# GAT source exponentials: spread over the partitions by DMA through a DRAM scratch, instead of by matmuls and copies

## Chip, cores, metric

The kernel runs on one core of one Trainium2 chip. The metric is the time of one execution in device microseconds (us).

## The reference

`x` is 16 batches of 1024 nodes by 256 channels, `adj` a 1024 x 1024 adjacency. Four layers follow one another, each on a layer norm of `x` and added to `x`. Layers 0, 1 and 3 are graph attention (GAT); layer 2 is a transformer block with the adjacency as mask.

```python
# layers 0 and 1 (one head), layer 3 the same for 4 heads of 64 channels
h = matmul(relu(layernorm(x)), W)
e = leaky_relu((h @ a1)[:, :, None] + (h @ a2)[:, None, :])   # source of row i + target of column j
att = softmax(where(adj > 0, e, -big), axis=-1)
x = x + act(matmul(att, h))                                   # relu or elu
```

With `s = h @ a1` and `d = h @ a2`, exp(leaky_relu(s_i + d_j)) is, up to a factor of i that cancels in the softmax, max(exp((alpha-1) s_i), exp((1-alpha) d_j)) * exp(alpha d_j). The kernel computes the three exponentials once per node. Each weight then is one max and one multiply with the mask.

## The kernel before

The exponentials `e` come out with the nodes on the partitions. For the weights, the targets j stay on the partitions, but the source values of 512 rows i have to lie along the free dimension, the same on all partitions: a row `r`. Making `r` is the part that the change replaces.

```python
        def see_gat(s):                       # once a stage, when the last e is there
            H = s.heads
            i = {0: 0, 1: B, 3: 2 * B}[s.layer] + s.b
            nc.gpsimd.tensor_copy(s.v[:, :, :, s.hs], s.e[:, :, 2 * H :])
            # ... two reductions for a range check

        def gat_front(s, n, h, box):          # one item: 512 rows of one head
            # ...
            def spread_source():
                rp = ps_sc.tile([P, HALF], F32, tag="sc", name="rp")
                for i in range(TH):           # 4 matmuls of 128 columns: column of e, made wide, times identity
                    nc.tensor.matmul(
                        rp[:, i * P : (i + 1) * P], lhsT=s.e[:, n * TH + i, h : h + 1].to_broadcast([P, P]),
                        rhs=ident, start=True, stop=True,
                    )
                box["r"] = work.tile([P, HALF], F32, tag="r", name="r", bufs=2)
                nc.scalar.copy(box["r"], rp)

            def weights(j):                   # 8 an item, on VectorE
                # ...
                nc.vector.scalar_tensor_tensor(
                    box[j // 2][:, j % 2, :], box["r"], s.e[:, j, H + h : H + h + 1], mask[:, j, cols], ALU.max, ALU.mult
                )
            return [spread_source] + [lambda j=j: weights(j) for j in range(NT)]

        def gat_back(s, n, h, box):           # 4 groups of 8 products: 257 columns (one head) or 65 (layer 3)
            # ...
                    nc.tensor.matmul(
                        av[:, : s.hs + 1], lhsT=box[j // 2][:, j % 2, i * P : (i + 1) * P], rhs=s.v[:, j, h, :],
                        start=(j == 0), stop=(j == NT - 1),
                    )
        # ...
        for i, (s, front, _) in enumerate(items):        # when each piece is emitted
            lead = 1 if s.layer == 2 else 8 if s.heads == 1 else 4
            for f, piece in enumerate(front):
                slot = first_slot[i] - lead + f * lead // len(front)
                (early if slot < 0 else due[slot]).append((s, piece))
        # ...
            for fs, piece in due[at_slot]:
                settle(fs)                    # drains the way in of stage fs before its first piece
                piece()
```

A *stage* is one layer of one batch. Stages of two batches alternate: layers 0, 1, 2, 3 of b and b+1, a *pair*, eight pairs in all. The *way in* of a stage (statistics, norm, transpose, projection, exponentials) is emitted in small steps between the products of the stage before. `settle` emits at once whatever of it is left.

## Time and profile before

In what follows PE is TensorE (PEld its weight loads), DVE VectorE, ACT ScalarE, POOL GpSimd and SP SyncE. `av` are the products, `rp` the spreads, `pm` the projections and `tp` transposes, by the names of the tiles that they write. Each fp32 matmul leaves two records in a trace, so a group of 8 products is 16 records.

| | before |
|---|---|
| median (lowest to highest) | 5569.73 us (5540.11 to 5572.35), 3 runs |
| profiled run | 5551.8 us, granted clock 0.951 |
| PE, DVE, ACT busy | 90%, 71%, 34% |

The prediction below shows the chain, the stretches of one pair and the groups concerned. The row of granted clock in the view of 40 slices (tenths of full speed, 9 is 90% or more):

```profile
PEclk9999999999999999998999999998999999999998
```

### The profile page before, as it was taken

What the parts mean: (1) busy time and instruction counts of PE and PEld (TensorE: products, weight loads), DVE (VectorE), ACT (ScalarE), POOL (GpSimd) and SP (SyncE); (2) the same over time, 40 slices, a digit from 0 to 9 for tenths busy, and PEclk for the clock granted to TensorE, in tenths of its full rate; (3) what the DMA queues carried; (4) which work ended last, traced back from release to release, by engine and by line L of the source; (5) the groups of instructions that cost most, each with busy time, mean ns of one, the idle gap of its engine ahead of it and who ended that gap; (6) DMA issues with size and microseconds to landing.
All of it is one profiled execution on the core that took longest, in us unless ns stands there. A gap on an engine that the chain in (4) does not pass through costs nothing.

```text
span 5551.8 us, 71153 instructions
## 1 busy us (share of the span) xinstructions
PE 4978.5 (90%) x27266; PEld 3127.0 (56%) x27266; DVE 3932.2 (71%) x7928; ACT 1905.7 (34%) x3345; POOL 1437.2 (26%) x2120
## 2 busy tenths in 40 slices
PE   4988899879998899988999889998899988999888
PEld 3832598226972279622795228852288423983248
DVE  4557885668757687576875678756786567865777
ACT  2344323442234422344223441234413443234430
POOL 1213322223222232123331232312323033231330
PEclk9999999999999999998999999998999999999998
DMA  2000000000000000000000000000000000000000
GB/s 79 1 1 1 3 29 1 1 1 5 27 1 1 1 7 26 1 1 1 16 16 1 1 1 16 16 1 1 1 16 16 1 1 1 20 5 1 1 1 17
DMA packets 40714, 45.92 MB, mean 8 GB/s; under 512 B 4144, under 2 KB 39088, under 8 KB 40368
## 3 DMA queue, kind: packets, MB, share of 16 engines
q1 hardware_dynamic: 35200, 37.75, 2.0%
q8 instruction: 218, 3.57, 0.3%
q10 hardware_dynamic: 5168, 3.54, 0.3%
q14 instruction: 128, 1.05, 0.1%
HBM read 24.51 MB, written 16.78 MB: 7 GB/s over the span
## 4 chain that ended last, share of the span: by engine, by line
PE 62%; DVE 30%; ACT 5%; issue 1%; POOL 1%; DVEq 0%; DMA 0%; ACTq 0%; POOLq 0%
PE av L561 25%; PE pm L461 14%; DVE pe L646 13%; PE sc L638 9%; PE acc L657 8%; DVE p L548 5%; ACT pe L644 4%; PE tp L456 3%; PE rp L538 3%; DVE st L445 2%; DVE y L713 1%; PE tpo L681 1%; DVE y L750 1%; DVE y L596 1%; DVE y L712 1%
## 5 line engine op out<-in xcount | busy, mean ns | idle before, releaser
L561 PE MATMUL av<-v,p 128*128 128x65 f32 (+1 forms) x12288 | 1968.5, 314 | 11.9 <-DVE y L596 10.5
L561 PEld LDWEIGHTS av<-v,p 128*128 128x128 f32 x12288 | 1748.4, 196 | 129.3 <-PE av L561 12.7
L646 DVE TENSOR_TENSOR pe<-pe,mask_pos 128x1024 f32<-128x1024 f32 x1024 | 1235.4, 1247 | 727.2 <-ACT pe L644 726.2
L644 ACT ACTIVATE pe<-sc 128x1024 f32<-128x1024 f32 x1024 | 992.9, 1022 | 767.8 <-PE sc L638 759.8
L657 PE MATMUL acc<-pe,v 128*33 128x512 f32 x4096 | 1058.4, 640 | 0.0
L449 POOL TENSOR_SCALAR rstd<-stats 128x1 f32<-128x1 f32 x768 | 411.4, 536 | 2410.7 <-DVE stats L447 2076.7
L548 DVE SCALAR_TENSOR_TENSOR p<-r,e,mask_pos 128x512 f32<-128x512 f32 x1280 | 917.3, 750 | 85.6 <-ACT r L543 84.6
L638 PE MATMUL sc<-qT,kT 32*128 32x512 f32 x4096 | 664.7, 708 | 0.0
L450 POOL TENSOR_TENSOR rstd<-rstd,minus_half 128x1 f32<-128x1 f32 x768 | 618.9, 806 | 64.0
L657 PEld LDWEIGHTS acc<-pe,v 128*33 128x33 f32 x4096 | 204.5, 115 | 674.0 <-issue 477.9
L461 PE MATMUL pm<-l_wx,hT 128*128 128x259 f32 (+1 forms) x1536 | 435.9, 410 | 11.8 <-ACT hT L457 11.8
L461 PEld LDWEIGHTS pm<-l_wx,hT 128*128 128x128 f32 x1536 | 288.5, 199 | 153.4 <-ACT hT L457 66.8
L574 DVE RECIPROCAL inv<-av 128x1 f32<-128x1 f32 x768 | 125.7, 164 | 320.1 <-PE av L561 315.8
L456 PE MATMUL tp<-ident,xn 128*128 128x128 f32 x1024 | 201.1, 281 | 156.2 <-DVE xn L473 146.5
L689 POOL TENSOR_TENSOR y<-y,z 128x256 f32<-128x256 f32 x128 | 100.7, 787 | 923.2 <-DVE z L685 923.2
L493 ACT ACTIVATE e<-pm 128x3 f32<-128x3 f32 (+1 forms) x384 | 67.5, 176 | 759.1 <-PE pm L461 759.1
L638 PEld LDWEIGHTS sc<-qT,kT 32*128 32x128 f32 x4096 | 186.5, 198 | 237.0 <-issue 146.5
L456 PEld LDWEIGHTS tp<-ident,xn 128*128 128x128 f32 x1024 | 130.0, 147 | 301.8 <-issue 117.5
L457 ACT ACTIVATE hT<-tp 128x256 f32<-128x256 f32 x512 | 194.5, 383 | 257.2 <-PE tp L456 257.2
L456 PE MATMUL tp<-ident,y 128*128 128x128 f32 x256 | 64.0, 337 | 230.9 <-DVE y L713 230.9
L473 DVE TENSOR_SCALAR xn<-x,stats,rstd 128x256 f32<-128x256 f32 x512 | 248.5, 485 | 14.8 <-PE tp L456 8.3
L543 ACT COPY r<-rp 128x512 f32<-128x512 f32 x192 | 112.2, 585 | 403.0 <-PE rp L538 331.2
(83 smaller groups left out, 4215.3 us busy)
## 6 DMA issues: line engine op xcount, KB each, us to landing
x<-in_x_dram SPq DMA_DIRECT2D x16, 1024.0 KB, 5.2
out_dram<-x SPq DMA_DIRECT2D x64, 256.0 KB, 2.1
edges<-in_adj_dram SPq DMA_DIRECT2D x8, 512.0 KB, 5.0
qkv_sb<-in_L_gnn_w_qkv_dram ACTq DMA_DIRECT2D x1, 768.0 KB, 6.5
l_wx<-in_L_gnn_W_dram ACTq DMA_DIRECT2D x2, 256.0 KB, 4.1
ab<-in_L_gnn_a_dram ACTq DMA_DIRECT2D x4, 128.0 KB, 4.1
w_sb<-in_L_gnn_w_dram ACTq DMA_DIRECT2D x2, 256.0 KB, 6.9
g_sb<-in_L_gnn_ln_g_dram ACTq DMA_DIRECT2D x2, 128.0 KB, 6.5
```

The costliest lines, as they stand in the source:

```text
L449: nc.gpsimd.tensor_scalar(r, stats[:, 1:2], EPS, None, ALU.add)
L450: nc.gpsimd.tensor_tensor(r, r, minus_half, ALU.pow)
L456: nc.tensor.transpose(tp[:, k, :], src[:, k * P : (k + 1) * P], ident)
L457: nc.scalar.activation(dst[:, :, t * P : (t + 1) * P], tp, func)
L461: nc.tensor.matmul(dst, lhsT=lhsT[:, k, :], rhs=rhs[:, k, :], start=(k == 0), stop=(k == KC - 1))
L473: nc.vector.tensor_scalar(xn, xs[s.b][:, t, :], box["m"], box["r"], ALU.subtract, ALU.mult)
L548: nc.vector.scalar_tensor_tensor(box[j // 2][:, j % 2, :], box["r"], s.e[:, j, H + h : H + h + 1], mask[:, j, cols], ALU.max, ALU.mult)
L561: nc.tensor.matmul(av[:, : s.hs + 1], lhsT=box[j // 2][:, j % 2, i * P : (i + 1) * P], rhs=s.v[:, j, h, :], start=(j == 0), stop=(j == NT ...
L638: nc.tensor.matmul(sc[:, hh, :], lhsT=s.kT[r0 : r0 + D2, g, j * P : (j + 1) * P], rhs=s.qT[r0 : r0 + D2, g, cols], start=True, stop=True,)
L644: nc.scalar.activation(p, sc, AF.Exp, scale=SCALE2)
L646: nc.vector.tensor_tensor(p, p, m, ALU.mult)
L657: nc.tensor.matmul(s.acc[pair][hh * 64 : hh * 64 + D2 + 1, :], lhsT=s.v[:, j, h, :], rhs=box[pair][:, hh, :], start=(j == 0), stop=(j == N ...
```

## The change

The intent is to free TensorE of 768 small matmuls and ScalarE of 192 copies: a stage's source exponentials are written to a DRAM scratch as rows, and each row is read back with a stride of 0 over the partitions. Since a DMA was expected to take longer to land than the matmuls and the copy, the read is issued 4 (one head) or 3 (four heads) slots before the old place of the spread; a slot is one group of products in layer 3 and half a group in layers 0 and 1.

```diff
+        dram = ctx.enter_context(tc.tile_pool(name="dram", bufs=3, space=bass.MemoryType.DRAM))
...
+                    self.rows = dram.tile([self.heads, N], F32, tag="rows", name="rows")
...
         def see_gat(s):
+            for h in range(H):
+                nc.sync.dma_start(
+                    out=s.rows[h : h + 1, :].rearrange("o (t p) -> p (o t)", p=P), in_=s.e[:, :, h]
+                )
...
             def spread_source():
-                rp = ps_sc.tile([P, HALF], F32, tag="sc", name="rp")
-                for i in range(TH):
-                    nc.tensor.matmul(
-                        rp[:, i * P : (i + 1) * P], lhsT=s.e[:, n * TH + i, h : h + 1].to_broadcast([P, P]),
-                        rhs=ident, start=True, stop=True,
-                    )
                 box["r"] = work.tile([P, HALF], F32, tag="r", name="r", bufs=2)
-                nc.scalar.copy(box["r"], rp)
+                nc.sync.dma_start(out=box["r"], in_=s.rows[h : h + 1, cols].to_broadcast([P, HALF]))
...
             lead = 1 if s.layer == 2 else 8 if s.heads == 1 else 4
+            if s.layer != 2:
+                slot = first_slot[i] - lead - (4 if s.heads == 1 else 3)
+                (early if slot < 0 else due[slot]).append((s, front.pop(0)))
```

## The prediction

> **What bounds the kernel now.** Sixteen batches go in eight pairs; each pair passes layer 0 (b, b+1), layer 1, layer 2, layer 3, so one pair takes about 690 us of the 5551.8. I read first the busy tenths in slices, which repeat eight times, then the chain that ended last, then the table of stretches for one pair, since the averages (PE 90%, DVE 71%) mix stages with different limits.
>
> From the page, the chain:
>
> ```profile
> PE 62%; DVE 30%; ACT 5%; issue 1%; POOL 1%; DVEq 0%; DMA 0%; ACTq 0%; POOLq 0%
> PE av L561 25%; PE pm L461 14%; DVE pe L646 13%; PE sc L638 9%; PE acc L657 8%; DVE p L548 5%; ACT pe L644 4%; PE tp L456 3%; PE rp L538 3%; DVE st L445 2%; DVE y L713 1%; PE tpo L681 1%; DVE y L750 1%; DVE y L596 1%; DVE y L712 1%
> ```
>
> The matmuls that the change removes (rp, L538) stand on it with 3%; the copy that follows them (L543) does not appear. Where they stand is told by the table of stretches of one pair. Its columns are the stretch and its length, then busy us of PE, PEld, DVE, ACT, POOL, the granted clock, DMA share, GB/s. The four rows are layer 3 of batch b, layer 3 of b+1, the layers 0 and 1 of the next pair (their first 179 us), and layer 2.
>
> ```profile
> 628.00:717.00 89.00, 81.98 (x612) 76.28 (x611) 77.31 (x200) 17.93 (x46) 34.17 (x51) 0.96 0.02 7
> 717.00:791.00 74.00, 73.15 (x618) 72.22 (x618) 68.41 (x165) 15.03 (x36) 12.08 (x17) 0.98 0.09 30
> 791.00:970.00 179.00, 178.21 (x873) 147.48 (x873) 106.99 (x261) 53.90 (x139) 48.64 (x83) 1.00 0.03 10
> 980.00:1300.00 320.00, 269.64 (x1244) 84.29 (x1240) 226.31 (x338) 142.84 (x186) 83.62 (x111) 0.93 0.00 1
> ```
>
> Layers 0 and 1 are bound by PE alone (178.2 of 179; DVE 60%): a PE microsecond saved there is saved. Layer 3 is bound by PE and DVE together (b: 92 and 87%; b+1: 99 and 92%): what PE gives up is soon asked for by DVE. Layer 2 hardly has this change in it.
>
> The groups and waits that the change touches:
>
> ```profile
> L538 PE MATMUL rp<-ident,e 128*128 128x128 f32 x1536 | 219.2, 290 | 8.9 <-ACT pe L644 8.9
> L543 ACT COPY r<-rp 128x512 f32<-128x512 f32 x192 | 112.2, 585 | 403.0 <-PE rp L538 331.2 <-DVE p L548 62.5 <-DVE st L445 6.1
> L548 DVE SCALAR_TENSOR_TENSOR p<-r,e,mask_pos 128x512 f32<-128x512 f32 x1280 | 917.3, 750 | 85.6 <-ACT r L543 84.6
> DVE p L548 <- ACT r L543: 116.1, 105, 2.0
> ```
>
> and PE in order in layer 1:
>
> ```profile
> 836.48 0.38 PE L456 MATMUL tp<-ident,xn 128*128 128x128 f32 x2
> 836.70 1.06 PE L538 MATMUL rp<-ident,e 128*128 128x128 f32 x8
> 837.59 1.91 PE L561 MATMUL av<-v,p 128*128 128x257 f32 x8
> ```
>
> The sum 219.2 us counts overlapping ends. From start to start one spread costs PE 837.59 - 836.70 = 0.89 us, with 192 of them 171 us, which is the chain's 3%. The last wait line says that DVE stood 116 us, 105 times, waiting for a spread row; 1.1 us each.
>
> **What the Trainium skill says.** "DMA: Bandwidth & Descriptors", Rules for kernel authors: a strided last dimension becomes one descriptor per element. So one write of a row (1024 values of 4 B, out of a strided tile) is 1024 packets. No DMA before has this in volume. The same page, Anatomy of one DMA, gives a fixed cost of about 2 us, mostly the receipt; the trace agrees in kind (32 KB broadcasts of ab land in 3.0 us, 256 KB stores in 2.1, 256 KB loads of l_wx in 4.1). The same page, Two DMAs through the same engine are not ordered: a read of what a DMA wrote has to wait for the completion semaphore, so write and read add up. The instruction list of the changed kernel shows such waits on each first read; no run yet gives the time. "TensorE: Matmul & The Clock Gate", Part 1: PE idleness lowers the clock for a window. The trace agrees: after 0.85 us of PE idle at 740.1 us the next spread took 1.98 us instead of 1.06, and that 10 us stretch shows 0.83. Small waits in layer 3 thus cost more than their length.
>
> **The change part by part.**
>
> *Removed from PE, layers 0 and 1.* 2 spreads per batch and layer, 4 x 16 = 64, times 0.89 us = 57 us, in a PE-bound stage: gain 57.
>
> *Removed from PE and DVE, layer 3.* 8 spreads per batch, 128 in all, 114 us of PE time. But in b+1 DVE has 68.4 us of work in 74: at best 5.6 us can go, I take 4. In b, most slices are DVE-bound by the tail of layer 2, with PE full only around 660 to 680; DVE waits for r there only 1.6 us; I take 3. Together 7 us x 8 pairs = 56. The ceiling, DVE at 100% in b+1 and 5 in b, would be 85.
>
> *Removed at the seam of layers 2 and 3.* rp borrows a score buffer; PE waited for ACT before it 24.4 us in 16 places, and the spread itself sits in the latency chain of layer 2. I take 15, choosing not to add all of it since the next score matmul inherits part of the wait.
>
> *Removed from ACT.* 192 copies of 0.585 us = 112 us; ACT is at 34% and not on the path: 0 by itself.
>
> *Added, DMA.* 96 row writes and 192 reads of 256 KB (50 MB). The scalar queue's 5168 mostly small packets took 0.1% of 16 engines' span, 89 us, or 17 ns each (9 to 26 with the rounding). A row is 64 packets per engine, 1.1 us (up to 1.7); landing about 3.0 + 1.1 = 4 us; four rows about 7.4. A read is estimated at 3 to 5 us. In the steady state r of an item can be asked for when DVE ends the item two before, and is needed one item later: 8 products of 0.72 us and 4 pairs of small operations of 0.4 us, 7.3 us. That hides it, save when a 1 MB load of x (5.2 us) is ahead in the rings.
>
> *Moved: the slot of the spread.* It is issued 4 slots (one head) or 3 slots (four heads) earlier, and a stage's way in must be finished (the schedule is drained) before its first spread. In layer 1 this pulls two steps of the way in together: PE waits for one transpose to be copied, about 0.7 us, twice a pair: 8 pairs x 1.4 = 11, and about 6 once at the start. In layer 3 of b+1 six steps are drained at once instead of three, so a chain statistics, POOL (1.55 us), norm, transpose, projection stands bare: about 3 us x 8 = 24. (Before, this drain already cost DVE about 4 us at 714.)
>
> *Added wait.* After that drain come 4 writes of rows and the first read behind them: 7.4 + some 3 us, against some 5 to 7 us of DVE work left of the item before. About 4 us x 8 = 32. For layer 3 of b, and for layer 0, the rows are long written: 0. For layer 1 there are 4 slots of about 2.2 us plus DVE slack: 0.
>
> Sum: -57 - 56 - 15 + 11 + 6 + 24 + 32 = -55. I shade it to -60, since the clock should gain a little with the shorter couplings, and predict 5570 - 60 = 5510 us.
>
> **The rivals.** (a) *Full gain*: all 171 us of rp and part of the 116 us of DVE waits go, since the PE-to-ACT-to-DVE round trip in every item was the true bound of layer 3. For it: the waits are exposed in front of DVE. Against: DVE is busy 92% in b+1, so the waits are worth 6 us a pair. It would give some 5420, faster by 2.7%. (b) *DMA latency takes the place of the wait*: if the element-wise row writes cost several times my 17 ns, or if reads land in over 7 us, DVE would wait for r at each item of layer 3. For it: thousands of 4-byte packets have no precedent in this trace. Against: the reads are long rows, and two buffers give a whole item of lead. With 2 us on each of 128 items it would be +256, minus the 57 of layers 0 and 1 and the seam: about 5700. (c) *DVE is the bound in layer 3 and nothing is gained there*, with the settling cost paid: -57 - 15 + 73, the time of before within 0.2%.
>
> **Range and chances.** Between (c) at about 5570 and a little under the ceiling of layer 3 without added waits (-57 - 85 - 15 + 17 = -140, 5430) lies most of what I hold likely; with run to run scatter of half a per cent (5540 to 5572) I set 5430 to 5580. Two per cent is 111 us: faster than 5458 needs layer 3 near its ceiling and a free seam, 0.2. Slower by 2% needs (b) in full: 0.07. Within 2%: 0.73.
>
> **What would show each step right or wrong.** In the changed profile: layers 0 and 1 of a pair still have PE at 99% and are shorter by about 7 us less 1.4 (the right sign of the first term). Layer 3 of b+1: length 74 falls to some 70, DVE busy goes to 95% or more, PE drops under 95%; if PE stays at 99% and the stretch is 66, rival (a) holds. The waits list must have no "DVE p <- ACT r"; in its place there should be a wait of DVE for the DMA of r, with few entries (about one per pair, 3 to 5 us each); a hundred entries would be rival (b). The landing of rows should be about 4 us for one and 7 to 8 for four; over 12 us proves my packet estimate wrong. The drain at the end of layer 3 of b should show DVE idle of 6 to 8 us where it had 4. The prediction goes wrong mostly by the cost of 4-byte packets and by how far DVE-bound slices of layer 3 give back what PE saves.

## The result, and the profile after

The changed kernel takes 6107.82 us (median of 4 runs, 6094.63 to 6112.29) against 5567.05 us (4 runs) before: ratio 1.0978, 95% interval 1.0939 to 1.1018. It is slower by 9.8%, and the prediction's range ends 528 us below it. Ratios here are the mean time of one kernel's fast runs over that of the other's of the same rounds, so not quite the ratio of the medians quoted.

The granted clock and the chain, from the page of the kernel after:

```profile
PEclk9999779997799978988689886999769997699875
...
PE 59%; DVE 26%; DMA 7%; ACT 5%; issue 1%; POOL 0%; DVEq 0%; SPq 0%; ACTq 0%
PE av L562 29%; PE pm L463 12%; DVE pe L647 12%; PE sc L639 8%; PE acc L658 7%; DVE p L549 4%; ACT pe L645 3%; DMA rows<-e 3%; DMA r<-rows 3%; PE tp L458 3%; DVE st L447 2%; PE tpo L682 1%; DVE xn L475 1%; DVE y L751 1%; DVE y L714 1%
```

Two things are new. The clock falls to between 0.5 and 0.7 once in every pair (mean 0.861, before 0.951), and DMA stands on the chain with 7%. The spread matmuls are gone from it, but the products `av` went from 25% of a shorter span to 29% of a longer one. Their group, before and after, and the waits around it after (columns: busy us, mean ns of one, idle before; for a wait, us in total, times, longest):

```profile
L561 PE MATMUL av<-v,p 128*128 128x65 f32 (+1 forms) x12288 | 1968.5, 314 | 11.9 <-DVE y L596 10.5
...
L562 PE MATMUL av<-v,p 128*128 128x65 f32 (+1 forms) x12288 | 2389.3, 363 | 163.4 <-DVE y L597 148.9
```

```profile
DVE p L549 <- DMA r<-rows: 234.7, 34, 20.8
PE av L562 <- DVE y L597: 148.9, 17, 19.7
```

The same 12288 records of products take 2389 us of busy time instead of 1968. VectorE waits 235 us for rows, in 34 places only, and up to 20.8 us at a time. The landings, from the list of DMA issues (count, KB each, median us to landing):

```profile
r<-rows SPq DMA_DIRECT2D x192, 256.0 KB, 3.6
...
rows<-e SPq DMA_DIRECT2D x96, 4.0 KB, 13.0
```

A read of 256 KB lands in 3.6 us, a write of 4 KB of single elements in 13.0. These are medians over the landings that the trace tells: 23 of the 192 reads and 10 of the 96 writes (8.3 to 18.9 us). The chain in order of time shows the worst place, the start of layer 3 of batch b+1 (start, length, what):

```profile
755.58 16.28 DMA rows<-e
771.86 0.02 SPq L544
771.88 0.05 issue
771.93 9.26 DMA r<-rows
781.19 0.03 issue
781.21 1.41 DVE p L549 x2
...
783.17 51.44 PE av L562 x240
```

Four rows land after 16.3 us (a fifth, of the next pair's layer 0, had been issued 2.2 us before them), the first read 9.3 us later; VectorE stands 20 us and TensorE 19. This can be read as a stall. The last line is something else. 240 records of products take 51.44 us, 0.21 us each, where they took 0.11 before. The stretches show it (columns as in the prediction):

```profile
790.00:800.00 10.00, 10.00 (x49) 10.00 (x49) 6.72 (x15) 0.63 (x1) 0.00 (x0) 0.50 0.07 23
800.00:810.00 10.00, 10.00 (x49) 10.00 (x49) 6.71 (x16) 0.63 (x1) 0.00 (x0) 0.50 0.07 23
```

TensorE is busy all the time, VectorE is not, nothing waits, and the clock is at half for 50 us. It comes back some 11 us after wider matmuls have joined, the projections `pm` of 259 columns (the timeline of PE):

```profile
834.83 3.51 PE L562 MATMUL av<-v,p 128*128 128x65 f32 x16
838.13 2.04 PE L463 MATMUL pm<-l_wx,hT 128*128 128x259 f32 x4
...
850.94 1.90 PE L562 MATMUL av<-v,p 128*128 128x65 f32 x16
852.67 1.10 PE L463 MATMUL pm<-l_wx,hT 128*128 128x259 f32 x4
```

The same 16 records take 3.51 us at 834 and 1.90 at 850.

To compare kernels by stage I cut each trace by the order of the products (every stage has a fixed number of them: 128 records in layers 0 and 1, 512 in layer 3), from the first product of a stage to that of the next, and added the eight pairs up; "3, b" and "3, b+1" are layer 3 of the first and second batch of the pairs. Half-speed products are records of layer 3 (8192 in all) that start 180 to 260 ns after the one before, where at full clock it is about 109. The table holds the experiments too, for what follows; us throughout.

| profiled run | layers 0+1 | layer 2 | 3, b | 3, b+1 | span | clock | half-speed products |
|---|---|---|---|---|---|---|---|
| before | 1360 | 2678 | 770 | 633 | 5552 | 0.951 | 386 |
| after | 1405 | 2680 | 1083 | 822 | 6111 | 0.861 | 4409 |
| e1 unread spreads added to after | 1426 | 2677 | 971 | 698 | 5893 | 0.916 | 1273 |
| e2 before without any spread | 1313 | 2682 | 883 | 715 | 5706 | 0.892 | 3268 |
| e3 e2 + unread spreads in layer 3 | 1313 | 2686 | 765 | 602 | 5482 | 0.955 | 249 |
| e4 before, only the slots moved | 1389 | 2686 | 885 | 645 | 5708 | 0.925 | 889 |
| e5 after, rows written in runs | 1371 | 2673 | 897 | 747 | 5796 | 0.887 | 2958 |
| e6 e5 + unread spreads in layer 3 | 1371 | 2679 | 811 | 651 | 5621 | 0.947 | 546 |
| e7 e3 with 64-column matmuls | 1314 | 2693 | 944 | 682 | 5738 | 0.915 | 1464 |
| e8 e3 with a quarter of them | 1313 | 2707 | 810 | 669 | 5606 | 0.916 | 1537 |
| e10 one of three versions faster than before | 1325 | 2674 | 787 | 610 | 5504 | 0.946 | 303 |

(The start of the program, 105 to 120 us, is the rest of each span.) Of the 559 us of difference between the two profiled runs, 502 are in layer 3, 45 in layers 0 and 1, 10 at the start, 2 in layer 2. In layer 3, the half-speed products took 420 us more than before (460 against 40, each counted as its excess over 109 ns), TensorE's idle time grew by 147 (217 against 70), and the removed matmuls gave back 128 x 0.89 = 114. That makes 453 of the 502; the rest I did not itemise (the other matmuls at half clock are in it).

### The profile page after: what moved, and what is told of

Read it like the earlier page. It is cut to its first block, busy times and chain, and to the rows that moved or that the text cites. A ratio compares the mean times of both kernels' runs of the same rounds, so it can differ in the third digit from the quotient of the medians.

```text
span 6110.5 us, 68391 instructions
## 1 busy us (share of the span) xinstructions
PE 5308.7 (87%) x25730; PEld 3408.0 (56%) x25730; DVE 3968.0 (65%) x7928; ACT 1802.6 (29%) x3153; POOL 1441.0 (24%) x2120
## 2 busy tenths in 40 slices
DMA packets 168192, 96.48 MB, mean 16 GB/s; under 512 B 107056, under 2 KB 142000, under 8 KB 167856
## 4 chain that ended last, share of the span: by engine, by line
PE 59%; DVE 26%; DMA 7%; ACT 5%; issue 1%; POOL 0%; DVEq 0%; SPq 0%; ACTq 0%
PE av L562 29%; PE pm L463 12%; DVE pe L647 12%; PE sc L639 8%; PE acc L658 7%; DVE p L549 4%; ACT pe L645 3%; DMA rows<-e 3%; DMA r<-rows 3%; PE tp L458 3%; DVE st L447 2%; PE tpo L682 1%; DVE xn L475 1%; DVE y L751 1%; DVE y L714 1%
## 5 line engine op out<-in xcount | busy, mean ns | idle before, releaser
L562 PE MATMUL av<-v,p 128*128 128x65 f32 (+1 forms) x12288 | 2389.3, 363 | 163.4 <-DVE y L597 148.9
L562 PEld LDWEIGHTS av<-v,p 128*128 128x128 f32 x12288 | 2183.5, 245 | 291.0 <-issue 174.4
L463 PE MATMUL pm<-l_wx,hT 128*128 128x259 f32 (+1 forms) x1536 | 470.4, 436 | 33.8 <-ACT hT L459 33.8
L463 PEld LDWEIGHTS pm<-l_wx,hT 128*128 128x128 f32 x1536 | 305.3, 212 | 192.8 <-ACT hT L459 96.7
L475 DVE TENSOR_SCALAR xn<-x,stats,rstd 128x256 f32<-128x256 f32 x512 | 259.8, 507 | 31.9 <-POOL rstd L452 24.4
L463 PE MATMUL pm<-hT,qkv_sb 128*128 128x512 f32 x512 | 244.6, 600 | 0.4
```

What stands on the lines that cost most here:

```text
L463: nc.tensor.matmul(dst, lhsT=lhsT[:, k, :], rhs=rhs[:, k, :], start=(k == 0), stop=(k == KC - 1))
L475: nc.vector.tensor_scalar(xn, xs[s.b][:, t, :], box["m"], box["r"], ALU.subtract, ALU.mult)
L562: nc.tensor.matmul(av[:, : s.hs + 1], lhsT=box[j // 2][:, j % 2, i * P : (i + 1) * P], rhs=s.v[:, j, h, :], start=(j == 0), stop=(j == NT ...
```

## The experiments

Theory A: the products of layer 3, 65 columns wide, cannot bring a lowered clock back by themselves; the spread matmuls, 128 columns wide and one set in every item, did this in passing. Theory B: the clock is only low because TensorE stands still in DMA stalls. Theory C: stalls alone make the loss. Beside these, the element-wise write and the moved slots had to be sized. Kernels e2, e3, e7 and e8 compute with ones in place of `r` and are wrong on purpose; all others were correct.

### e1: the spread matmuls put back, unread

```diff
+            def warm():
+                rp = ps_sc.tile([P, HALF], F32, tag="sc", name="rp")
+                for i in range(TH):
+                    nc.tensor.matmul(rp[:, i * P : (i + 1) * P], ...)      # as before; nobody reads rp
-            return [spread_source] + [...]
+            return [spread_source, warm] + [...]
```

> The changed kernel (6108 us) with the spread matmuls put back in their old slots, written to PSUM and never read; the DMA path stays. Theory A (the narrow products of layer 3, 65 columns wide, cannot lift a lowered TensorE clock by themselves, and the 128-column spread matmuls did): the granted clock goes from 0.86 back to 0.93 or more, and the time falls by 250 to 400 us to about 5700 to 5850, though 171 us of PE work are added. Theory B (the clock is only low because PE stands still in the DMA stalls): the stalls stay, so the clock stays under 0.88 and the time is the same or longer, 6100 to 6250 us. Theory C (the DMA stalls alone make the loss): same as B.

Measured: 5893.19 us (ratio to before 1.0558, 1.0503 to 1.0614), clock 0.916. Adding 171 us of TensorE work that nobody reads made the changed kernel some 215 us faster. That contradicts B and C. Theory A had the direction, but its numbers were too hopeful (5700 to 5850, clock 0.93): the long stalls are still there (VectorE waits 256 us for rows, up to 20.0 at a time), and the clock is lost after them anew: 29 low periods in layer 3, 499 us together.

### e2 and e3: no spread at all, and unread spreads in layer 3 alone

```diff
# e2, from the kernel before
             def spread_source():
-                rp = ...; 4 matmuls; copy
+                box["r"] = r_one              # a constant tile of ones
# e3, from e2
+                if H > 1:
+                    rp = ps_sc.tile([P, HALF], F32, tag="sc", name="rp")
+                    ...                       # the 4 matmuls as before, unread
```

> The kernel before with the spread taken out and nothing in its place: the products read one constant tile of ones (wrong result on purpose), no DMA, no spread matmuls, no copies, slots as before. Theory A: the clock in layer 3 still drops to 0.5 for tens of us after each gap, mean clock 0.90 or less, and the time is not better than before: 5550 to 5750 us. Theories B and C (only DMA stalls hurt): clock 0.94 to 0.96 and 5400 to 5450 us, the full 171 us of spreads gained.

> As e2 (ones in place of the spread row, wrong on purpose), but in layer 3 the spread matmuls run unread in their old place. Theory A: clock 0.95 again, and time about before minus 57 us (spreads of layers 0 and 1) minus some of the 116 us that DVE waited for r: 5420 to 5500 us, faster than e2. Theories B and C: slower than e2 by up to 114 us.

Measured: e2 5703.38 us (1.0225, 1.0183 to 1.0267), clock 0.892; e3 5484.85 us (0.9842, 0.9797 to 0.9887), clock 0.955. They ran on the same chip in the same rounds. This is the decisive pair: e2 has no DMA of rows, no stall, no matmul and no copy for the spread, and is slower than before; adding 114 us of unread matmuls to it makes it 219 us faster. The same place in both, by the timeline of PE. In e2:

```profile
718.85 14.40 PE L556 MATMUL av<-v,p 128*128 128x65 f32 x128
733.78 29.22 PE L556 MATMUL av<-v,p 128*128 128x65 f32 x144 [0.53 <-DVE y L591]
762.80 0.63 PE L458 MATMUL tp<-ident,xn 128*128 128x128 f32 x2
763.22 3.51 PE L556 MATMUL av<-v,p 128*128 128x65 f32 x16
```

and in e3:

```profile
725.27 5.47 PE L563 MATMUL av<-v,p 128*128 128x65 f32 x48
731.44 1.97 PE L563 MATMUL av<-v,p 128*128 128x65 f32 x16 [0.70 <-DVE y L598]
733.25 1.11 PE L542 MATMUL rp<-ident,e 128*128 128x128 f32 x8
734.20 7.26 PE L563 MATMUL av<-v,p 128*128 128x65 f32 x64
```

Up to the gap both run the products at full speed (128 records in 14.4 us in e2). Then e2 waits 0.53 us for VectorE and runs the next 144 records in 29.2 us; e3 waits 0.70 us, longer, and in this pair goes on at full speed. The other pairs show that this is not the rule: in e3 the clock fell after this same gap of 0.7 us in five of the eight pairs, but for 3.4 us each time. In e2 it fell after the gap of 0.5 us in six of seven pairs (the seventh lost it 7 us later, after a gap of 1.0 us), for 34 to 51 us. So the spreads do not keep a gap from costing the clock; they bring it back at once. Nor do they work by removing gaps: TensorE's idle time in layer 3 is not smaller in e3 than in e2 (some 76 against 63 us).

So narrow products can keep a full clock (they do before the gap), but a short gap is enough to lose it, and they do not bring it back. In all traces of this case each loss in layer 3 came after at least 0.57 us of idle within the 3.4 us before it; not every such gap was followed by a loss. I looked up how each low-clock period of layer 3 ended, by what ran in its last 3.5 us. In e2 there are 24 such periods, 831 us together; 23 end with a projection, and the last runs to the end of the program. Before there are 22, only 156 us together, and 14 of them end with a spread. After there are 36, 1208 us: 33 end with a projection, 2 with the 257-column products of the next layer 0, and one runs to the end. That a projection is there could be chance, since projections are often there. So cut e2's low periods into windows of 3.4 us: of 39 windows with a projection, 23 were the last of their period; of 205 without one, only the last of the program was.

### e4: the earlier slots alone

```diff
# the scheduling lines of the change, on the kernel before; spread by matmuls and copy as before
+            if s.layer != 2:
+                slot = first_slot[i] - lead - (4 if s.heads == 1 else 3)
+                (early if slot < 0 else due[slot]).append((s, front.pop(0)))
```

> The kernel before with one part of the change alone: the spread is issued 4 (one head) or 3 (four heads) slots earlier, still by matmuls and copies. The prediction charged 41 us to this (11 + 6 + 24): 5590 to 5620 us. Rival: the earlier spread lets DVE go without waiting for r (116 us of waits), so it gains: 5480 to 5560 us.

Measured: 5710.69 us (1.0225, 1.0162 to 1.0289), clock 0.925: about 130 us lost, 41 were expected, so the estimate missed by a factor of three; and the rival is refuted. By the table 29 us are in layers 0 and 1, 115 in layer 3 of b, 12 in that of b+1. I took the intervals between the starts of the 32 groups in layer 3 of b, mean of the pairs: the row of eight in which the way in of b+1 is drained takes 28.5 us instead of 22.9, so 5.6 x 8 = 45 us for the drain. The first three rows of eight take 82.2 instead of 73.3, 71 us for the eight pairs; there half-speed products went up (611 against 94), and their excess over 109 ns accounts for 54 of the 71 us. The spread no longer stands where it stood at the start of layer 3. That this alone moved the clock is my reading; no run separates it.

### e5 and e6: rows written in contiguous runs, and unread spreads on top

```diff
# e5, from the kernel after; e is laid out [P, 3H, NT]
-            for h in range(H):
-                nc.sync.dma_start(out=s.rows[h : h + 1, :].rearrange("o (t p) -> p (o t)", p=P), in_=s.e[:, :, h])
+            turned_e = ps_mm.tile([P, HALF], F32, tag="mm", name="tpe")
+            nc.tensor.transpose(turned_e[: NT * H, :P], s.eh[:, :H, :].rearrange("p h t -> p (h t)"), ident)
+            flat_e = ...                                      # [NT * H, P] in SBUF
+            nc.scalar.copy(flat_e, turned_e[: NT * H, :P])
+            nc.sync.dma_start(out=s.rows.rearrange("h (t p) -> (h t) p", p=P), in_=flat_e)
# e6: e5, and the unread spreads of e1 for H > 1
```

> The changed kernel with one part replaced: the source exponentials of a stage are turned by one TensorE transpose and one ScalarE copy, and written to the scratch by one DMA of 512 B runs (8 or 32 of them) instead of 1 or 4 DMAs of 1024 single elements each. Reads and slots stay. If the landing of the element-wise writes (13 us) makes the DMA stalls, landing falls to 2 to 4 us, DVE waits for r fall from 235 us to under 100, and the time falls by 120 to 220 us to 5890 to 5990; the clock stays under 0.90 (theory A), since no wide matmuls come back. Theory B (the low clock comes from the stalls): clock above 0.93 and 5500 to 5600 us.

> e5 and in layer 3 the spread matmuls put back unread, in the old slots. Theory A: both losses mended; what is left against e3 (5485) is the earlier slots (e4: +130 us): clock 0.92 to 0.94, 5560 to 5680 us, at least 200 us faster than e5. Theory B: slower than e5 by up to 114 us.

Measured: e5 5804.07 us (1.0441, 1.0385 to 1.0497), clock 0.887; e6 5630.93 us (1.0146, 1.0096 to 1.0196), clock 0.947. The waits and issues of e5:

```profile
DVE p L551 <- DMA r<-rows: 40.9, 15, 5.0
```

```profile
rows<-flat_e SPq DMA_DIRECT2D x16, 16.0 KB, 1.4
```

One write of 16 KB in runs of 512 B lands in 1.4 us, and VectorE's waits for rows fall from 235 us to 41. (The 1.4 is the median of the 7 landings of 16 that the trace tells.) The ratio to before went from 1.0978 to 1.0441: some 300 us, more than the 120 to 220 expected. The clock is low for less time as well (34 periods of layer 3, 720 us together, against 36 and 1208; 2958 half-speed products instead of 4409). Yet the clock stays at 0.887 with nearly no stall left, against B; only the unread spreads of e6 bring it back, and make it 173 us faster though they are work (at least 200 were expected).

### e7 and e8: narrower, and fewer, unread matmuls

```diff
# e7, from e3
-                    for i in range(TH):        # 4 of 128 columns
+                    for i in range(2 * TH):    # 8 of 64 columns, rhs=ident[:, i % 2 * 64 : (i % 2 + 1) * 64]
# e8, from e3
-                    for i in range(TH):
+                                               # one matmul of 128 columns
```

> e3 with the same number of unread columns in layer 3, but as eight matmuls of 64 columns instead of four of 128 (ones in place of the spread row, wrong on purpose). If it is the width of the moving operand that lifts the clock (theory A), these act like the 65-column products: clock 0.90 or less as in e2 (0.892), and time above e2 (5703), 5700 to 5850 us. Rival A2 (any extra matmuls, or the break in the stream, do it): clock 0.95, 5480 to 5560 us as e3.

> e3 with only one of the four 128-column unread matmuls for each item of layer 3 (wrong on purpose). If a lift needs enough wide work inside a short stretch, one does too little: clock 0.89 to 0.92 and 5620 to 5720 us, near e2. If a single wide matmul is enough: clock 0.95 and 5400 to 5460 us, faster than e3 by up to 86 us (three quarters of 114).

Measured: e7 5743.85 us (1.0318, 1.025 to 1.0386), clock 0.915; e8 5639.24 us (1.0163, 1.0116 to 1.021), clock 0.916. They ran on another chip than e2 and e3, where before took 5552 us instead of 5578. The same columns in halves of 64 do not do it, as e7's timeline of PE shows at the start of layer 3:

```profile
633.25 3.62 PE L542 MATMUL rp<-ident,e 128*128 128x64 f32 x16
636.66 7.04 PE L563 MATMUL av<-v,p 128*128 128x65 f32 x32
```

The unread matmuls themselves run at half clock and the products after them too. Of e7's 17 low-clock periods in layer 3 none ended with narrow matmuls alone: a projection was in the last 3.5 us of 16, and one ran to the end of the program. The clock was above the 0.90 that I expected (there were fewer half-speed products than in e2, 1464 against 3268), so extra matmuls are not quite without effect: they change how often the clock is lost. That rival, "any extra matmul", would have made it as fast as e3, and it was 259 us slower. One wide matmul in place of four (e8) gives a time between e2 and e3, as expected, but it never brought the clock back: of e8's 24 low periods in layer 3, 23 ended with a projection in their last 3.5 us and one ran to the end. So the amount of wide work in a short stretch counts. Why e8's low periods are shorter than e2's (463 us together, against 831) is not shown.

### e9, e10, e11: versions meant to beat both

All three write rows as e5 does, one step after the last exponentials (e11 in layers 0 and 1 alone). e9: the first spread of a stage by matmuls and copy in its old slot, so that nothing is drained earlier; the others by DMA; in layer 3 the spread matmuls run on unread. e10: the same, but with the first item of layers 0 and 1 by DMA as well. e11: layer 3 exactly as before, and only the second item of a stage of layers 0 and 1 by DMA.

```diff
+            sources = [spread_copy] if by_pe else [spread_dma] + ([spread_pe] if H > 1 else [])
# by_pe: e9  n == 0 and h == 0;  e10  n == 0 and h == 0 and H > 1;  e11  [spread_copy] if H > 1 or n == 0 else [spread_dma]
-            if s.layer != 2:
+            if s.layer != 2 and not first_of[i]:
                 slot = first_slot[i] - lead - (4 if s.heads == 1 else 3)
```

> A version meant to beat both: the first spread of each stage by matmuls and copy in its old slot (so no earlier draining); all others by DMA, read early, from rows written in one contiguous DMA one step after the last values; in layer 3 the spread matmuls run on, unread. If the three losses found (element-wise writes, lowered clock, earlier slots) are all there is, the clock is 0.95 and the time is before minus about 25 us (layers 0 and 1) minus about 36 us (layer 3, as e3 against before): 5480 to 5530 us. If a further loss sits in the DMA reads, 5550 or more.

> e9, but in the one-head layers the first item of a stage also comes by DMA, in its old slot. If DVE's slack in layers 0 and 1 hides the landing (some 6 us), faster than e9 by up to 28 us: 5455 to 5510 us. If not, layers 0 and 1 gain nothing and it is equal or slower: 5500 to 5560 us.

> The lean version: layer 3 exactly as before (matmuls and copies); in layers 0 and 1 only the second item of a stage by DMA. Expected before minus 28 us plus a few: 5530 to 5560 us, slower than e9 if the waits for r in layer 3 are worth something, equal if not.

Measured, in the same five rounds: e9 5533.91 us (0.9932, 0.9892 to 0.9973), e10 5522.20 (0.9920, 0.9888 to 0.9951), e11 5521.83 (0.9916, 0.9883 to 0.9949), before 5569.02. All three are faster than before by 0.7 to 0.8%, clear of the noise but small, and their intervals overlap, so none is shown better than the others. e9 and e10 ended above what they promised, and e11, the simplest, beat its range slightly. Layer 3 gains little by DMA even when everything is mended: the sum of its two columns is 1397 us in e10 and 1403 before (and 1425 in the profiled run of e9, itself one of its slower ones).

## Why the prediction was wrong

**The step that failed first: the clock.** The prediction says "I shade it to -60, since the clock should gain a little with the shorter couplings". It had the sign wrong and the size out of sight. It cites the skill's page "TensorE: Matmul & The Clock Gate", Part 1, for "PE idleness lowers the clock", and even quotes the case of 740.1 us, where the clock fell after 0.85 us of idle. Two things are missing in that reading. The page's table speaks of an idle window of about 3.4 us, and the trace lost the clock after 0.85, so the trace did not agree on the length. And the prediction took the low clock to last "for a window"; it did not ask what ends it. At 740.1 us this was there to be seen:

```profile
740.12 1.97 PE L561 MATMUL av<-v,p 128*128 128x65 f32 x16 [0.85 <-DVE y L596]
741.93 1.98 PE L538 MATMUL rp<-ident,e 128*128 128x128 f32 x8
743.70 6.50 PE L561 MATMUL av<-v,p 128*128 128x65 f32 x50
```

The low period that began there lasted one window of 3.4 us, and the spread, the very thing that was to be removed, stood in it. Before, the clock fell at this place in all eight pairs and was low for 3.4 to 17.1 us. In the changed kernel low periods of 81.9 us, 24 windows, begin in the stall of four pairs. The runs put a number on it: with no spread and no DMA the kernel loses 2.2% (e2), with unread spreads in layer 3 it gains 1.6% (e3). In the changed kernel half-speed products cost 420 us more than before; not all of this is the missing spreads alone, since the stalls made more occasions to lose the clock (e5 against after), and the moved slots some (e4).

**The second step: "17 ns each", "landing about 3.0 + 1.1 = 4 us; four rows about 7.4", "About 4 us x 8 = 32".** The page "DMA: Bandwidth & Descriptors", Rules for kernel authors, was used rightly: one descriptor for each element. The trace agrees: packets under 512 B went from 4144 to 107056, and 96 rows of 1024 elements are 98304. The price of a packet came from a misread line. The page of the kernel before has

```profile
q10 hardware_dynamic: 5168, 3.54, 0.3%
```

for the scalar queue; the 0.1% is that of another queue, q14. With 0.3% the same sum gives an estimate of 52 ns for a packet, 6.3 us for one row and 16.2 for four, and an added wait some 70 us larger, which would still have left the prediction over 500 us short. Measured: 8.3 us for a single row with nothing beside it, 16.3 for four, and the read behind them 9.3 us instead of 3.6. That 16.2 comes so near is luck. The packets of that queue are mostly of 256 B and more. And the packets are not where a row's time goes: of the row issued alone at 979.06 us the trace records all element packets, of some 7 ns each, between 979.96 and 980.64, but it landed at 987.32. The term that was mis-sized is this stretch from the last packet to the landing, 6.7 us; no run shows what fills it. VectorE stood 18 to 21 us at the start of layer 3 of b+1 (10 in the last pair) instead of the 4 that I had added, 148 for the eight pairs instead of 32.

**The third step: the moved slots, "11", "6", "24", 41 us together.** e4 measured about 130. The drain in layer 3 was 45 instead of 24, layers 0 and 1 gave 29 instead of 11; the other 71 us are in the first three quarters of layer 3 of b, where the estimate had no term.

**What held.** Layers 0 and 1: 57 us predicted; e2 and e3 give 1360 - 1313 = 47 for taking the spreads away. In the changed kernel itself the sign is turned, 1405 against 1360: e4 puts 29 us of that on the slots, and e5, which writes in runs and has 1371, puts 34 on the element-wise writes; some 29 us more are not itemised. Layer 3, 56 us: e3, where matmuls stay and only waits and copies are gone, gives 36; its full size cannot be had since the matmuls are needed. The seam with layer 2, 15 us: no gain, layer 2 is the same within 8 us in e2 and e3. The 24.4 us from which the 15 were taken counted one set of waits twice, 8.9 us of PE and 15.5 of its weight loads. The reads, "3 to 5 us", landed in 3.6 and were hidden in the steady state as said. Of the rivals, (b) named the DMA, but as a wait at each item of layer 3 (a hundred entries); the list has 34, long ones at the starts of stages. (Its sum is off too: 256 - 57 - 15 added to 5570 is about 5750, not 5700.) No rival named the clock, which is the larger half.

**What stays open.** What the clock's governor counts is not shown, only what lifted it here: sets of four spreads of 128 columns, projections of 256 columns or more and the products of 257, and never products or unread matmuls of 64 or 65 columns. Every narrow matmul here has a weight load of its own, and e7 doubles the loads as it halves the width. So whether it is the width that counts, or the ratio of columns to weight loads, is not separated; a run with narrow matmuls that share their weights could tell. Of e4's 71 us in the first three quarters 54 stand in half-speed products; why the clock is lost more often there is argued, not shown. Half-speed products in e7 fell without a wide matmul added; the runs do not say why the clock is lost less often there (17 low periods in layer 3 against 24 in e2).

## What to carry to other kernels

Before you remove matmuls from a stage, look at what remains: if it is a stream of narrow ones, those that you remove may be what keeps or restores the clock, and "PE busy 100%" will not show it; read the granted clock by stretches and the time of one and the same group at different places. A short experiment that keeps the work and throws away its result (e3) tells this apart from all waiting. For rows through DRAM, turn the data on chip first, so that the DMA writes contiguous runs, and do not let the first use in a stage wait for a write that has only just been issued (18 to 21 us a pair here).

## What the Trainium skill lacked or had wrong

- "TensorE: Matmul & The Clock Gate", Part 1, says that the clock is full after "≥1 busy SHORT window (~3.4µs sustained)". Here TensorE was busy without a gap and stayed at half: 51.4 us from 783 us on, within a low period of 81.9 us. The stream was fp32 matmuls of 65 columns, one weight load each. The page gives no warning that a stream of such narrow matmuls may not bring the clock back; with sets of four spreads of 128 columns, or with projections of 259, among them it came back.
- The same page's rule is "no PE-idle gaps >~3.4µs"; for shorter ones it tells of a kernel that idles often between bursts, without a length. Here single short gaps were enough: 0.53 us (e2) was followed by 34 to 51 us of half clock in a stream of narrow products, and 0.70 us (e3) by 3.4 us of it in five of eight pairs. The low periods were multiples of 3.4 us, and granted shares were 1.0 or 0.5 only, in agreement with the page's window and its two states.
- "DMA: Bandwidth & Descriptors", Rules for kernel authors, says that a strided last dimension becomes one descriptor per element. It gives no time to landing for such a write. Here 1024 elements of 4 B from SBUF to DRAM landed in 8.3 us alone and in 13.0 in the median of the 10 writes whose landing the trace tells, though the packets of the row alone were over 1.6 us after its issue; 16 KB in runs of 512 B landed in 1.4.
- The same page, Anatomy of one DMA, gives the fixed cost of one DMA as about 2 us, in a section on DMAs issued from GpSimd; the prediction left that out. These here were issued from SyncE, so it is no contradiction that the contiguous write of e5 landed 1.4 us after its issue. Reads of 256 KB took 3.2 to 3.6.
